# A perceiver block on one core: experts multiplied ahead of the next transposes, settling transposes pinned, and splits moved at both ends of the way up

## The chip, the core and the metric

The kernel runs on 1 core of one Trainium2 chip. The metric is the device time of one execution in microseconds (us), here the median of three runs. The engines are TensorE (PE, with its weight loads as PEld), VectorE (DVE), ScalarE (ACT), GpSimd (POOL) and SyncE (SP, which issues most DMAs).

## What is computed

One block in float32: a cross attention onto a masked context, a causal self attention with low-rank queries and keys, and a feed-forward part. 32 sequences of 64 tokens, 512 features.

```python
x = x + xattn(layernorm(x), ctx, mask)
x = x + attn(layernorm(x), ...)        # 16 heads; ends with out.reshape(..., 2048) @ wo.T + bo
h = layernorm(x)
y = square(relu(h @ up_w)) @ down_w    # 512 -> 2048 -> 512
y = y + (h @ expert_weight) * top2_sum(h @ gate_w)
x = x + layernorm(y) * ln_gamma + ln_beta
```

The matrix product of the attention's output with `wo` is called the way out, `h @ up_w` the way up and `... @ down_w` the way down. `expert_weight` and `gate_w` side by side are "the expert".

## The kernel before

**Tiling.** The 2048 tokens are 8 blocks of 256 (`NB`, `TB`). The three large products (way out, way up, way down) are made with seven products of submatrices in place of eight: sums of submatrices are formed on POOL, and each float32 operand is split into a high part (rounded to float32r, an ACT copy, L147) and a low part (the rest, a DVE subtraction, L149). A product of two split operands takes three matmuls: high x high, low x high, high x low. `split` does the pair of instructions and takes `pins`: an ACT and a DVE instruction behind which the two are issued. `after(ins)` orders the instructions of a block behind `ins` on its engine; it adds no semaphore. The order on each engine is otherwise a scheduler's, which follows the program's order by priority and issues ahead what it holds ready.

**The way out** runs over 64 units (`out_units`): a unit is one (block, k) and one call of `seven`, 21 matmuls of 128x256 (L723, L725, L726). k goes over the eight weight slots in the order of `ORDER`. `read_pair` reads a unit's operand with a DMA into one of the rooms of `ccp`, up to four units ahead; `left(u)` splits it into one of three `hl` rooms, two units ahead. `put_slot(k, "wo" | "up" | "down")` splits a weight into its slot (two ACT and two DVE instructions). At a block's last k its four PSUM banks are summed by `combine` (ACT L160, DVE L162 to L168), then `o_sum` and `o_norm` take the layer norm; POOL takes the root (L127), DVE writes `on` (L139).

**Transposes and experts.** `o_t(blk)` turns a normed block with eight transposes (L985) in two PSUM rooms of the pool `ps_t`, which has four rooms, and splits it into `oh` and `ol`; both have one room. It also copies it to `oT`, which ACT's queue stores to `xT_d` for the way up. `o_expert(blk)` multiplies `oh`, `ol` with the expert by `mm3` (L179 to L181): two halves of 128 tokens, each 12 matmuls of 264 columns and 12 of 256, 48 matmuls in four rooms of `ps_t`. DVE takes the two largest gate values (L1016) and adds them (L1018), ACT scales both parts into `mo` (L1021, L1022) and issues the store of `mo` to `mo_d` (L1023). `o_expert` is a generator: its first `yield` stands before the second half's scaling. Before, `o_t` for blocks 0 to 6 comes after the units in `TURN_AT`, `o_expert` after those in `MULT_AT`. Block 7's `o_t` and `o_expert` follow the loop.

**The rooms.** `o_act` (`ap`) holds `beb`, `mo`, `xt`, `o`, `p1`, `xn`, `oh`, `ol`, one room each, placed in the order of their first allocation. `mos` allocates `mo` ahead of the loop. When the way out ends, `pc.close()` frees the pool, and `f_act` (`fp`) is placed over it: three rooms for `uo`, the sums of the way up, and two for `p1`. A write to a new room waits until the tiles that lay there are done with.

**The way up** runs over 4 rounds (b, 512 tokens each) and in each over the 8 weights of `ORDER`: `up_seven` is 42 matmuls (L1156) into the four banks of one of two PSUM pools, then `combine`, ReLU and square on ACT (L1226, L1227), sums on POOL, stores to `h_d`. The first eight settling transposes are issued by `settle` (L713): transposes of 128 columns whose result is overwritten. `right(b, part)` splits the features of a round; round 0's four parts are split at the end of the way out and just behind it. The first weights of the way up are split inside the way out: `UP_PUT` names the units of block 7 after which `ORDER[0]` and `ORDER[1]` are split; `ORDER[2]` follows the last `o_t`; the others come in round 0, three weights ahead.

**The end of the way up and the way down.** In the last round the weights of the way down are split (`ORDER[n - 2]` for n = 2 to 6) and its first three operands by `left(0)`, `left(1)`, `left(2)` at n = 3, 5 and 6. The way down is again 64 units of 21 matmuls; `left(u + 3)` runs three units ahead. Four settling transposes stand after unit 4 and after unit 31 (`SETTLE_AT`), pinned behind the unit before (`ends`).

Of the kernel before, what the change touches and what calls it, by code (L numbers as in the profile page):

```python
# [9 lines left out]
FP = mybir.dt.float32  # L10
# [39 lines left out]

BARE_FIRST, BARE_LAST = ORDER[:5], ORDER[2:]

READ_AT, SLOT_AT = (1, 2, 4, 5), (3, 5, 7, 9, 11)
EXPERT_AT = (15, 16, 17, 18)
TURN_AT = (19, 22, 28, 34, 42, 50, 58)
MULT_AT = (21, 25, 31, 39, 47, 55, 63)

FEATURES_AT = (2, 4)
UP_READ, UP_PUT = (1, 2, 5, 6, 7), (3, 5)

BETA_AT = 60

# [24 lines left out]
def perceiver_block(ctx: ExitStack, tc: tile.TileContext, x, mem, mask, wq_a, bq_a, qnw, wq_b, bq_b,  # L87
# [53 lines left out]
    def after(ins):  # L141
        return tc.issue_after(ins.ins) if ins is not None else ExitStack()
# [32 lines left out]
    def mm3(ps, pairs):  # L175

        n = len(pairs)
        for j, (ah, al, bh, bl) in enumerate(pairs):
            nc.tensor.matmul(ps, ah, bh, start=(j == 0), stop=False)  # L179
            nc.tensor.matmul(ps, al, bh, start=False, stop=False)  # L180
            nc.tensor.matmul(ps, ah, bl, start=False, stop=(j == n - 1))  # L181


    with ExitStack() as mla:
# [409 lines left out]
        with ExitStack() as pb:  # L594
# [57 lines left out]
            def put_slot(k, what, pins=(None, None)):  # L652

                hl, c, _ = read_slots.pop((what, k))
                h, l = hl or room_of(k, what)
                for a in (slice(0, 4), slice(4, 7)):
                    split(h[:, a], l[:, a], c[:, a], pins=pins)
                wts[k] = (h, l)
# [342 lines left out]

    def o_expert(blk, xh, xl, _):

        mo = mos.pop(blk, None) or ap.tile([P, 2, D], FP, tag="mo", name=f"mo{blk}")
        for tt in range(2):
            i = 2 * blk + tt
            sl = slice(tt * P, (tt + 1) * P)
            pes = []
            for c in (slice(256, NE), slice(0, 256)):
                pe = ps_t.tile([P, D], FP, tag="T", name=f"cpe{i}_{c.start}")  # L1010
                mm3(pe[:, 0 : c.stop - c.start], [
                    (xh[:, k, sl], xl[:, k, sl], wes[0][:, k, c], wes[1][:, k, c]) for k in range(NKD)
                ])
                pes.append(pe)
            t8 = sp.tile([P, 8], FP, tag="t8", name=f"t8{i}")
            nc.vector.max(t8, pes[0][:, 256:264])  # L1016
            gs = sp.tile([P, 1], FP, tag="gs", name=f"gs{i}")
            nc.vector.tensor_tensor(gs, t8[:, 0:1], t8[:, 1:2], ALU.add)  # L1018
            if tt:
                yield  # L1020
            nc.scalar.mul(mo[:, tt, 256:512], pes[0][:, 0:256], gs)  # L1021
            nc.scalar.mul(mo[:, tt, 0:256], pes[1][:, 0:256], gs)  # L1022
        nc.scalar.dma_start(mo_d[blk], mo)  # L1023
        yield

    xr, xc, xw = {}, {}, []

    def read_x(b, kk, room=None, behind=None):

# [37 lines left out]
                    ins = nc.scalar.copy(t[:, to], src)  # L1067
        return ins

    mos = {0: ap.tile([P, 2, D], FP, tag="mo", name="mo0")}  # L1070
    put_slot(ORDER[2], "wo")
    xt, xns, xT, x2s, dones, read = {}, {}, {}, {}, {}, 5
    for u, (blk, k) in enumerate(out_units):
# [38 lines left out]
            put_slot(ORDER[UP_PUT.index(u % 8)], "up", pins=low)  # L1112
        if u in TURN_AT:
            i = TURN_AT.index(u)
            xT[i] = o_t(i, xns.pop(i))
            if i == 0:
                xns[1] = o_norm(1, *xns[1], low[1])
# [8 lines left out]
                xt[blk + 1] = o_load(blk + 1)  # L1126
        if u == BETA_AT:
            o_beta(NB - 2, low[1], nc.gpsimd)
        if u in MULT_AT:
            i = MULT_AT.index(u)  # L1130
            scaled = o_expert(i, *xT.pop(i))
            next(scaled)
            if i < NB - 2:
                next(scaled)
    xT = o_t(NB - 1, xns.pop(NB - 1), lambda: next(scaled))
    for part in range(3):
        right(0, part, (dones[NB - 1][0], xT[2][1]))
    put_slot(ORDER[2], "up", pins=xT[2])
    for _ in o_expert(NB - 1, *xT):
        pass  # L1140
    pc.close()


# [2 lines left out]
    with ExitStack() as pu:  # L1146
# [3 lines left out]
        def up_seven(ps, k, b, n, steps):  # L1150
            wh, wl = (t[:, 0:7].rearrange("p a (k f) -> p a k f", k=2) for t in wts[k])

            def product(s, parts, first=False, last=False):
                i, j = SEVEN[s]
                for m, (kk, w, low) in enumerate(parts):
                    nc.tensor.matmul(  # L1156
                        ps[s // 2][:, s % 2], w[:, i, kk], xr[b, 2 * kk + low][:, j],
                        start=(first and m == 0), stop=(last and m == len(parts) - 1),
                    )

            most = [(0, wh, 0), (0, wl, 0), (0, wh, 1), (1, wh, 0), (1, wl, 0)]
            rest = [(1, wh, 1)]
            one, two = (0, 2, 4, 6), (1, 3, 5)
            late = None
            if n == 0:
                with after(settle(8, ps, wh[:, 0, 0], ident2, None) if b == 0 else None):
                    for s in one:
                        product(s, most, first=True)
            if n == 7:
                for s in one:  # L1170
                    product(s, rest, first=True)
                for s in (0, 2, 4):
                    product(s, most, last=True)
                for s in two:
                    product(s, rest, first=True)
                if b + 1 < NB // 2:
                    late = right(b + 1, 3)
            for s in range(7):
                if n == 0 and s in one:
                    product(s, rest, last=True)  # L1180
                elif n < 7:
                    product(s, most + rest, True, True)
                elif s in two or s == 6:
                    product(s, most, last=True)
                if s in (1, 3, 5, 6):
                    with after(late if s == 3 else None):
                        next(steps)
# [8 lines left out]
                nc.sync.dma_start(h_d[b][:, k, 3:7], w)  # L1196

        stores = []
        right(0, 3)
        behind = read_slot(ORDER[5], "up", behind=reads[-1])  # L1200
        for b in range(NB // 2):
            if b == NB // 2 - 1:
# [2 lines left out]
            for n, k in enumerate(ORDER):  # L1205
# [28 lines left out]
                    summed = sums(at, LEFT)  # L1234
                if b == 0 and n < 5:
                    put_slot(ORDER[n + 3], "up", pins=pins)
                if b == NB // 2 - 1 and 1 < n < 7:
                    put_slot(ORDER[n - 2], "down", pins=pins)
                if b == NB // 2 - 1 and n == 2:
                    for u in range(2):  # L1240
# [2 lines left out]
                    left(0, pins=(done[0], done[-1]))  # L1243
                if b == NB // 2 - 1 and n == 5:
                    left(1, pins=(done[0], done[-1]))
                if b == NB // 2 - 1 and n == 6:
                    left(2, pins=(done[0], done[-1]))
                if b == NB // 2 - 1 and n == 7:
                    read_pair(5, from_h)
                if stores and (b, n) != (NB // 2 - 1, 7):  # L1250
# [8 lines left out]
    with ExitStack() as pd:  # L1259
# [82 lines left out]
        for u, (blk, k) in enumerate(out_units):  # L1342
            if k == ORDER[0]:
                pss[blk] = banks(ps_f[DOWN.index(blk) % 2], f"dp{blk}")
            while read <= min(max(u + READ_AHEAD, 2 * u + 1), u + READ_FAR, last_unit):
                read_pair(read, from_h, room_for(read))
                read += 1
            for v in [v for v in bares if v <= u + SUM_AHEAD]:
                c = bares.pop(v)
                with after(pows[-1]):  # L1350
                    sums([c[:, 6]] + [c[:, d] for d in range(7)], LEFT)
# [14 lines left out]
                store_h(*stores.pop(0))  # L1366
            if u == 6:
                nc.sync.dma_start(gab, gamma.partition_broadcast(P))
            if u in (4, 6, 8):
                put_slot(ORDER[3 + u // 2], "down")  # L1370
            if u in (2, 4):
                read_slot(ORDER[5 + u // 2], "down")
            outs = [d for d in outs if step(d, low)]
# [52 lines left out]
```

## Time and profile before

| | us |
|---|---|
| median of 3 runs | 1103.37 |
| lowest and highest run | 1101.33, 1103.40 |
| the profiled execution's own time | 1098.9 |
| its span, first to last instruction | 1096.7 |
| attention and folding, 0 to about 551 | 551 |
| way out, about 551 to 773.1 | 222 |
| way up, 773.1 to 931.2 | 158 |
| way down and the end, 931.2 to 1096.7 | 165 |

In the stretch 553 to 773 PE is busy 212.9 of 220 us, from 773 to 931.2 157.6 of 158.2, and from there to the end 155.5 of 165.5, of which the last ten are the output's tail on DVE and ACT. The granted clock is 1.00 in all three.

Rows of a list of groups, a list of waits or an order of time read: start (us), duration, engine, line, operation, out<-in by the program's names, partitions x elements, count, and in brackets the idle time of that engine before it with what ended it. A row of a stretch reads: from:to, its length, the busy time of PE with the number of instructions that touch the stretch, then the granted clock, the DMA engines' share and GB/s. Matmul ends are modelled and matmuls overlap, so their starts are what tells a pace.

### The profile page before, as it was taken

What the parts mean: (1) busy time and instruction counts of PE and PEld (TensorE: products, weight loads), DVE (VectorE), ACT (ScalarE), POOL (GpSimd) and SP (SyncE); (2) the same over time, 40 slices, a digit from 0 to 9 for tenths busy, and PEclk for the clock granted to TensorE, in tenths of its full rate; (3) what the DMA queues carried; (4) which work ended last, traced back from release to release, by engine and by line L of the source; (5) the groups of instructions that cost most, each with busy time, mean ns of one, the idle gap of its engine ahead of it and who ended that gap; (6) DMA issues with size and microseconds to landing.
All of it is one profiled execution on the core that took longest, in us unless ns stands there. A gap on an engine that the chain in (4) does not pass through costs nothing.

```text
span 1096.7 us, 26072 instructions
## 1 busy us (share of the span) xinstructions
PE 1066.9 (97%) x10201; PEld 983.6 (90%) x10201; DVE 769.0 (70%) x1369; ACT 546.1 (50%) x1051; POOL 508.1 (46%) x691
## 2 busy tenths in 40 slices
PE   8999999999999999999998999999999999999996
PEld 6667777679999999999988999999999999999996
DVE  5666666657666666656787866667785658898786
ACT  4444444533433444434475544445676567755553
POOL 2333333326788778874570000003238970065671
PEclk9999999999999999999999999999999999999999
DMA  8867666343776778655487776779646689998672
GB/s 259 263 216 231 206 212 203 124 161 121 260 234 245 260 247 294 249 207 195 160 324 276 263 241 213 231 235 359 218 156 202 221 247 366 310 309 257 206 232 79
DMA packets 195386, 254.67 MB, mean 232 GB/s; under 512 B 18544, under 2 KB 140032, under 8 KB 195264
## 3 DMA queue, kind: packets, MB, share of 16 engines
q1 hardware_dynamic: 190704, 240.92, 67.0%
q10 hardware_dynamic: 3456, 8.39, 2.2%
q0 software_dynamic: 1104, 3.70, 0.9%
q8 instruction: 80, 1.31, 0.5%
q14 instruction: 42, 0.34, 0.1%
HBM read 146.67 MB, written 106.30 MB: 231 GB/s over the span
## 4 chain that ended last, share of the span: by engine, by line
PE 59%; DMA 10%; POOL 9%; DVE 8%; issue 7%; ACT 5%; SPq 1%; DVEq 0%; POOLq 0%; ACTq 0%
PE up L1156 9%; PE pss L773 5%; PE psq L179 4%; PE psq L180 4%; PE psq L181 4%; PE op L725 3%; PE op L726 3%; PE op L723 3%; PE psv L817 3%; DMA hd<-uo 2%; PE pse L179 2%; PE pse L181 2%; PE pse L180 2%; DMA x1d<-xt 2%; DMA vd<-vw 2%
## 5 line engine op out<-in xcount | busy, mean ns | idle before, releaser
L755 DVE SCALAR_TENSOR_TENSOR qe<-pse,bqp,cq 64x256 f32<-64x256 f32 x256 | 123.7, 483 | 76.5 <-PE pse L181 70.7
L1156 PE MATMUL up<-xr,wh_up 128*128 128x256 f32 x896 | 157.6, 280 | 0.6 <-DVE uo L168 0.6
L1156 PEld LDWEIGHTS up<-xr,wh_up 128*128 128x128 f32 x896 | 137.5, 189 | 1.0 <-issue 0.7
L725 PE MATMUL op<-wh_wo,hl 128*128 128x256 f32 x448 | 124.4, 279 | 3.7 <-DVE hl L149 3.7
L723 PE MATMUL op<-wh_wo,hl 128*128 128x256 f32 x448 | 124.0, 280 | 0.6 <-ACT hl L147 0.6
L725 PE MATMUL dp<-wh_down,hl 128*128 128x256 f32 x448 | 124.5, 278 | 0.0
L723 PE MATMUL dp<-wh_down,hl 128*128 128x256 f32 x448 | 124.4, 278 | 0.0
L726 PE MATMUL dp<-wl_down,hl 128*128 128x256 f32 x448 | 124.3, 277 | 0.0
L149 DVE TENSOR_TENSOR hl<-c,hl 128x896 fp32r<-128x896 f32 x84 | 94.3, 1126 | 42.3 <-ACT hl L147 42.0
L1156 PE MATMUL up<-xr,wl_up 128*128 128x256 f32 x448 | 123.7, 280 | 0.0
L726 PE MATMUL op<-wl_wo,hl 128*128 128x256 f32 x448 | 123.5, 277 | 0.0
L147 ACT CAST hl<-c 128x896 fp32r<-128x896 f32 x84 | 79.0, 942 | 77.7 <-PE op L726 38.0
L179 PE MATMUL psq<-qa_hi,qh 128*128 128x256 f32 x384 | 112.5, 293 | 0.0
L180 PE MATMUL psq<-qa_hi,ql 128*128 128x256 f32 x384 | 106.4, 277 | 0.0
L181 PE MATMUL psq<-qa_lo,qh 128*128 128x256 f32 x384 | 106.2, 276 | 0.0
L725 PEld LDWEIGHTS op<-wh_wo,hl 128*128 128x128 f32 x448 | 84.3, 188 | 4.8 <-DVE hl L149 4.7
L723 PEld LDWEIGHTS op<-wh_wo,hl 128*128 128x128 f32 x448 | 83.6, 188 | 1.5 <-ACT hl L147 0.8
L723 PEld LDWEIGHTS dp<-wh_down,hl 128*128 128x128 f32 x448 | 84.6, 189 | 0.0
L725 PEld LDWEIGHTS dp<-wh_down,hl 128*128 128x128 f32 x448 | 84.1, 188 | 0.4 <-DVE hl L149 0.4
L1156 PEld LDWEIGHTS up<-xr,wl_up 128*128 128x128 f32 x448 | 84.2, 188 | 0.0
L726 PEld LDWEIGHTS op<-wl_wo,hl 128*128 128x128 f32 x448 | 84.1, 188 | 0.0
L726 PEld LDWEIGHTS dp<-wl_down,hl 128*128 128x128 f32 x448 | 84.1, 188 | 0.0
(233 smaller groups left out, 3146.6 us busy)
## 6 DMA issues: line engine op xcount, KB each, us to landing
c<-vd SPq DMA_DIRECT2D x58, 448.0 KB, 4.2
cx<-in_ctx SPq DMA_DIRECT2D x32, 512.0 KB, 4.6
vd<-vw SPq DMA_DIRECT2D x29, 512.0 KB, 3.6
hd<-uo SPq DMA_DIRECT2D x107, 128.0 KB, 3.3
hd<-uw SPq DMA_DIRECT2D x21, 512.0 KB, 3.3
dcw<-hd SPq DMA_DIRECT2D x18, 448.0 KB, 5.6
vd<-v SPq DMA_DIRECT2D x30, 256.0 KB, 3.5
wd_wo<-pw_wo SPq DMA_DIRECT2D x8, 896.0 KB, 4.9
```

The costliest lines, as they stand in the source:

```text
L147: copy = nc.scalar.copy(hi, src)
L149: return copy, engine.tensor_tensor(lo, src, hi.bitcast(FP), ALU.subtract)
L179: nc.tensor.matmul(ps, ah, bh, start=(j == 0), stop=False)
L180: nc.tensor.matmul(ps, al, bh, start=False, stop=False)
L181: nc.tensor.matmul(ps, ah, bl, start=False, stop=(j == n - 1))
L723: first = nc.tensor.matmul(ps[s // 2][:, s % 2], h[:, a], wh[:, b], start=(k == 0 and s % 2 == 0), stop=False)
L725: nc.tensor.matmul(ps[s // 2][:, s % 2], l[:, a], wh[:, b], start=False, stop=False)
L726: ins = nc.tensor.matmul(ps[s // 2][:, s % 2], h[:, a], wl[:, b], start=False, stop=last)
L755: rope = nc.vector.scalar_tensor_tensor(qe[64 * a : 64 * a + 64, :], pe[r, :], bqp[r, p : p + 1], cq[r, a, :], ALU.add, ALU.mult,)
L773: nc.tensor.matmul(ps[64 * j : 64 * j + 64, pj, b, :], qs[2 * pj + j][a][:, sl], kT[:, a, kt], start=(a == 0), stop=(a == 1),)
L817: nc.tensor.matmul(o, kv[a, i, :], t[a, bp, :], start=True, stop=True)
L1156: nc.tensor.matmul(ps[s // 2][:, s % 2], w[:, i, kk], xr[b, 2 * kk + low][:, j], start=(first and m == 0), stop=(last and m == len(parts) ...
```

## The change

- `mos` goes: `mo` is allocated when the first `o_expert` runs.
- `MULT_AT` goes: `o_expert(i - 1)` runs whole directly ahead of `o_t(i)` for i = 1 to 6; block 6's stays after the last unit, its last scaling still between block 7's transposes and their copies.
- `ORDER[1]` of the way up is no longer split after the sixth unit of block 7 but behind the first three `right` parts: its ACT half pinned to the last `left`'s ACT copy, its DVE half to the last `o_t`'s low part. `ORDER[2]` moves from there to behind the fourth part, `right(0, 3)`.
- The way up's settling transposes become four, issued behind the last matmul of the last expert (`made[-1]`, kept as `ends`; `mm3` returns its last matmul).
- In the last round of the way up `ORDER[4]`'s split and `left(2)` go; `left(2)` is issued at unit 0 of the way down ahead of the others, `ORDER[4]` after unit 1.

```diff
-UP_READ, UP_PUT = (1, 2, 5, 6, 7), (3, 5)
+UP_READ, UP_PUT = (1, 2, 5, 6, 7), (3,)
-MULT_AT = (21, 25, 31, 39, 47, 55, 63)
...
-            nc.tensor.matmul(ps, ah, bl, start=False, stop=(j == n - 1))
+            ins = nc.tensor.matmul(ps, ah, bl, start=False, stop=(j == n - 1))
+        return ins
...
-        mo = mos.pop(blk, None) or ap.tile([P, 2, D], FP, tag="mo", name=f"mo{blk}")
+        mo = ap.tile([P, 2, D], FP, tag="mo", name=f"mo{blk}")
...
-                mm3(pe[:, 0 : c.stop - c.start], [
+                made.append(mm3(pe[:, 0 : c.stop - c.start], [
...
-    mos = {0: ap.tile([P, 2, D], FP, tag="mo", name="mo0")}
...
         if u in TURN_AT:
             i = TURN_AT.index(u)
+            if i:
+                for _ in o_expert(i - 1, *xT.pop(i - 1)):
+                    pass
             xT[i] = o_t(i, xns.pop(i))
...
-        if u in MULT_AT:
-            i = MULT_AT.index(u)
-            scaled = o_expert(i, *xT.pop(i))
+        if u == last_unit:
+            scaled = o_expert(NB - 2, *xT.pop(NB - 2))
             next(scaled)
-            if i < NB - 2:
-                next(scaled)
     xT = o_t(NB - 1, xns.pop(NB - 1), lambda: next(scaled))
     for part in range(3):
         right(0, part, (dones[NB - 1][0], xT[2][1]))
-    put_slot(ORDER[2], "up", pins=xT[2])
+    put_slot(ORDER[1], "up", pins=(low[0], xT[2][1]))
     for _ in o_expert(NB - 1, *xT):
         pass
+    ends = made[-1]
...
-                with after(settle(8, ps, wh[:, 0, 0], ident2, None) if b == 0 else None):
+                with after(settle(4, ps, wh[:, 0, 0], ident2, ends) if b == 0 else None):
...
-        right(0, 3)
+        put_slot(ORDER[2], "up", pins=(xT[2][0], right(0, 3)))
...
-                if b == NB // 2 - 1 and 1 < n < 7:
+                if b == NB // 2 - 1 and 1 < n < 6:
                     put_slot(ORDER[n - 2], "down", pins=pins)
...
-                if b == NB // 2 - 1 and n == 6:
-                    left(2, pins=(done[0], done[-1]))
...
+            if u == 0:
+                left(2)
...
-            if u in (4, 6, 8):
-                put_slot(ORDER[3 + u // 2], "down")
+            if u in (1, 4, 6, 8):
+                put_slot(ORDER[max(4, 3 + u // 2)], "down")
```

`settle`, which the change calls with another count and pin, is unchanged:

```python
def settle(n, ps, sta, one, behind):
    for i in range(n):
        with after(behind):
            behind = nc.tensor.transpose(ps[3][:, 1, 0:P], sta.bitcast(FP), one)
    return behind
```

More of the change, by code (lines that the diff above doesn't have):

```diff
@@ L1010, in o_expert @@
                 pe = ps_t.tile([P, D], FP, tag="T", name=f"cpe{i}_{c.start}")
-                mm3(pe[:, 0 : c.stop - c.start], [
+                made.append(mm3(pe[:, 0 : c.stop - c.start], [
                     (xh[:, k, sl], xl[:, k, sl], wes[0][:, k, c], wes[1][:, k, c]) for k in range(NKD)
-                ])
+                ]))
                 pes.append(pe)
@@ L1024, in o_expert @@
         yield
-    xr, xc, xw = {}, {}, []
+    xr, xc, xw, made = {}, {}, [], []
     def read_x(b, kk, room=None, behind=None):
```

## The prediction

> **What bounds the kernel now.** I read the page first, then TensorE's busy time in equal stretches, then the order of time on each engine round the edited places.
>
> ```profile
> span 1096.7 us, 26072 instructions
> PE 1066.9 (97%) x10201; PEld 983.6 (90%) x10201; DVE 769.0 (70%) x1369; ACT 546.1 (50%) x1051; POOL 508.1 (46%) x691
> ```
>
> TensorE (PE) sets the time. So an edit is worth only the PE waits that it ends, the matmuls it adds, or a change of the pace at which matmuls follow each other. That pace isn't constant. The next view counts the up matmuls (128x256) in four stretches of 33 us, with the granted clock at 1.00 in all:
>
> ```profile
> 774.00:807.00 33.00, 33.00 (x283) 1.00 0.46 147
> 811.00:844.00 33.00, 33.00 (x294) 1.00 0.61 203
> 850.00:883.00 33.00, 33.00 (x283) 1.00 0.63 206
> 896.00:929.00 33.00, 33.00 (x282) 1.00 1.07 355
> ```
>
> One matmul lasts 0.28 us and the edges count too, so a stretch is 33.28 us: 33.28/283 = 117.6 ns from start to start, against 33.28/294 = 113.2 ns. There are two paces, 4.4 ns apart. The order of time shows where they turn: 117.6 ns from 773.1 to the PE wait at 808, 113.2 to three short waits at 846.8 to 847.5, then 117.6 through the rest of the way up and five units of the way down, to 943.5. There four settling transposes stand, and behind them 532 matmuls take 60.28 us, 113.3 ns each. A wait can leave either pace behind it; the transposes of the way out and of the way down were each followed by the quick one.
>
> **The start of the way up.** The kernel issues eight settling transposes there, and they aren't where they would help:
>
> ```profile
> 764.82 1.08 PE L985 MATMUL ops<-ident,on 128*128 128x128 f32 x8 [1.02 <-DVE on L139]
> 765.75 0.49 PE L713 MATMUL up<-ident,wh_up 128*128 128x128 f32 x3
> 766.66 0.51 PE L179 MATMUL cpe<-we_hi,oh 128*128 128x264 f32 x2 [0.43 <-ACT oh L147]
> 767.01 0.60 PE L713 MATMUL up<-ident,wh_up 128*128 128x128 f32 x4
> 773.04 0.27 PE L713 MATMUL up<-ident,wh_up 128*128 128x128 f32 x1
> 773.07 0.36 PE L1156 MATMUL up<-xr,wh_up 128*128 128x256 f32 x1
> ```
>
> Seven ran inside or ahead of the last expert, in time that PE was waiting anyway; one stands before the first up matmul. The change issues four, behind the expert's last matmul. The four at 943.53 cost 0.36 us to the next matmul's start (943.89) and the row after it starts 0.20 instead of 0.12 us later, so about 0.11 each: three more on the path, **+0.3** (bounds 0 and +0.45). If they leave the quick pace, the 297 matmuls up to 808 gain 4.4 ns each, **-1.3** (bounds 0, if one more disturbance follows, and -1.3).
>
> The Trainium skill speaks against this part: "TensorE: Matmul & The Clock Gate", section "Back-to-back issue gap", gives a warm isolated gap of N/2.4 + 2.5 ns, 109 ns for 256 columns, as a single value. By that rule no transpose could change the pace, and this part would only cost its 0.3. The trace has 113.2 and 117.6 at a granted clock of 1.00, so the rows decide.
>
> **The room of the first sums.** `mo` is allocated second in `o_act` before, so the first `uo` of the way up lies over it. The change allocates `mo` last there. In the trace:
>
> ```profile
> 774.17 0.33 ACTq L1023 DMA_DIRECT2D mod<-mo  x1
> 780.10 0.69 DVE L162 TENSOR_TENSOR uo<-up,up 128x512 f32<-128x512 f32 x1 [4.67 <-ACT up L160]
> 808.87 0.48 PE L1156 MATMUL up<-xr,wh_up 128*128 128x256 f32 x2 [0.57 <-DVE uo L168]
> ```
>
> The store of the last `mo` takes 5.8 us to land, so 779.97. DVE then starts its first sum of the way up at 780.10, though PE had ended that sum's banks at about 777.3 (34 matmuls after 773.07, 0.118 each, and the last one's end). The page names ACT's copy, which came late by chance; the wait is for the store. Behind it DVE runs a cycle of 4.73 us per weight (its splits at 785.37, 790.10, 794.83, 799.56, 804.29), PE one of 42 x 117.6 = 4.94, or 4.75 at the quick pace. DVE is therefore never more than level, and the late start is still there at 808.02, where PE waits 0.85 - 0.11 = 0.74 us. Starting about 3 us sooner, while PE gains 1.3 on it, DVE has 1.7 in hand against the 0.74. **-0.7** (bounds 0 and -0.74). What is late next are ORDER[1]'s and ORDER[2]'s low halves, both moved behind the last transposes. On DVE a low half is 1.2 + 0.95 us; they fit in the 4.67 us of idle that stood there, and ORDER[1]'s ends about when the way up begins, 4.75 us before its second weight needs it.
>
> **The end of the way out.** ORDER[1]'s low half runs on DVE at 755.37 (2.63 us, two instructions), and the last block's first sum follows at 757.92. PE had ended the banks for it at about 757.0. Sum, norm and POOL's root hang on it, and the last transposes waited 1.02 us for `on`. With the split pinned behind the transposes the chain starts 0.9 sooner: **-0.9** (bounds 0 and -1.0, the whole wait).
>
> **Experts ahead of the transposes.** All 8 x 48 expert matmuls and 8 x 8 transposes stay; only their order against the units changes. Two waits go:
>
> ```profile
> 617.44 0.51 PE L179 MATMUL cpe<-we_hi,oh 128*128 128x264 f32 x2 [0.47 <-ACT oh L147]
> 755.50 0.39 PE L725 MATMUL op<-wh_wo,hl 128*128 128x256 f32 x1 [0.63 <-DVE hl L149]
> ```
>
> At 616.70 expert 0 waited for its own split (0.74 to the next start against 0.12): it now stands behind the rest of that unit, **-0.6**. At 754.60 a pair landed late (its read issued at 746.48 took 6.82 us). That read waited for a room that the split of unit 61 frees, and that split for unit 58's matmuls. Before, an expert of 5.76 us stood in front of units 56 to 58; now it stands behind them, so the read goes out about 5.8 us sooner against the same need: 0.90 - 0.11, **-0.8** (bounds +0.9, if a run of eight units without a pause meets a late pair elsewhere, and -0.8). The moved stores of `mo` stay on ACT's queue, ahead of the casts that follow the transposes; these casts have eight units of cover.
>
> **The end of the way up.** ORDER[4]'s split (DVE 2.1, ACT 1.8) and left(2) (1.08 and 0.94) leave the last block and come as first work of the way down (the pair for left(2) is still read at the old place, into its own room, and only holds it longer). In the stretch 931.2 to 943.4 DVE is busy 11.5 and ACT 11.7 of 12.2 us, so this is no free place: left(2) is due two units (4.8 us) in, and my queue of DVE ends it 0.5 us before; ORDER[4] is due 9.5 us in, and ends about 0.4 before. At the slow pace **0**; at the quick pace PE arrives 1.5 us sooner and could wait 1 to 1.5 us in all.
>
> **What the waits leave behind.** The second round (b = 1) ends with short waits: these six matmuls take 1.23 us, where five paces of 0.113 and one end of 0.28 are 0.85, so 0.38 is waiting.
>
> ```profile
> 846.59 1.23 PE L1156 MATMUL up<-xr,wh_up 128*128 128x256 f32 x6
> 943.53 0.60 PE L713 MATMUL dp<-ident,wh_down 128*128 128x128 f32 x4
> ```
>
> They come from POOL and ACT work of that round, which keeps its place relative to PE; I expect them again, and behind them either pace. The 815 matmuls from there to 943.5 are slow now: quick would give -3.6, less up to 1.5 of new waits. Half of 2.1 gives **-1.0** (bounds +1.5, if the second round's 327 turn slow, and -3.6). The 250 slow matmuls of the way down from 1035 are a throw of the same kind, 1.1 either way; I take 0.
>
> **Sum.** +0.3 - 1.3 - 0.7 - 0.9 - 0.6 - 0.8 - 1.0 = -5.0 us against this execution, 1098.9 us with 2.2 outside the span. It lies 4.5 under the median of 1103.37 (1101.33 to 1103.4). 4.5 us is 1000 matmuls at the other pace, so other executions probably drew worse; I take the difference off the median: **1098.4**.
>
> **Rivals.** (1) *The quick pace holds from 773 to the way down*: nothing disturbs PE at 847. The throw then gives -3.6 in place of -1.0: 1095.8. For it: behind transposes the pace stayed for up to 567 matmuls; against: the waits at 847 are no part of the change. (2) *DVE and ACT take the gain of the way up back*: they run 4.73 us per weight against 4.75, so PE only arrives to wait. Then only -0.9 - 0.6 - 0.8 + 0.3 remain: 1101.4, no change that can be told. Against it: DVE idles 4.67 us at the start. (3) *Slower: the transposes wait for rooms*. `ps_t` has four rooms, an expert fills all four, and transposes now follow at once. They wait if the second scaling of the expert's first half ends later than its own 48 matmuls, 5.76 us. For expert 5 it ended at 736.34, 5.07 us after 731.27; for expert 0 at 624.34, 6.90 after 617.44. It decides against the change from 4.0/6 = 0.67 us late at each of six turns; at expert 0's 1.14 it costs 6.8, net 1103.37 - 5.0 + 6.8 = 1105.2. Against it: five of six new places have no block's end beside them, which is what delayed DVE in both rows. (4) *It doesn't do what it says*: the order within PE is set by a scheduler, which had already moved the eight settling transposes; but the four now have an edge to hold them. I count it within (2).
>
> **How the numbers follow.** Forecast 0.54, (1) 0.17, (2) 0.16, (3) 0.13. A difference under 0.2%, 2.2 us, can't be told from none here. Faster is the forecast and (1), 0.71, less a little for the forecast's own upper end: 0.69. Same takes (2) and that: 0.17; slower 0.14. The forecast's own range is 1095.5 to 1101.3; for 8 in 10 it goes down to 1094.3 (all terms at their best ends and a kind throw in the way down) and up to 1103.5 (the terms halved and the second round slow).
>
> **What would show it.** Four settling transposes directly ahead of the first up matmul, and 294 matmuls in the first 33 us of the way up; DVE's first `uo` sum about 4 us after the first up matmul instead of 7; no wait near its 297th matmul; the last transposes within 0.3 us of the expert; no waits of expert 0 on `oh` or of the last unit on a pair. I'm wrong if transposes show waits on `mo` scalings, if the pace behind the four is 117.6, or if new waits stand in the first five units of the way down.

## The result and the profile after

The changed kernel takes **1109.91 us** (median of 4 runs, 1108.5 to 1110.55) against 1102.58 for the kernel before (median of 4, 1101.33 to 1103.4). The ratio is **1.0072, 95% interval 1.0044 to 1.0099**: slower by 0.7%. The forecast was 1098.4 with a range up to 1103.5, so both its sign and its range were wrong. The profiled execution took 1109.55 us against 1098.9.

The first two lines of the page of the changed kernel, the span and the busy times:

```profile
span 1107.3 us, 26052 instructions
...
PE 1072.2 (97%) x10197; PEld 987.5 (89%) x10197; DVE 766.8 (69%) x1369; ACT 545.3 (49%) x1051; POOL 498.5 (45%) x691
```

No work was added: DVE and ACT are busy 2.2 and 0.8 us less than before. The 10.6 us of span are time in which TensorE stood still or ran slower. By stage, from first matmul to first matmul: the way out from the first transposes took 159.5 instead of 158.4 us, the way up 165.7 instead of 158.1, the rest 168.3 instead of 165.5; what lies ahead of the first transposes took 0.75 less. So 7.6 us of the loss are in the way up and 2.8 behind it. (The granted clock of the kernel before in its last stretch is 0.98, not 1.00: 1.00 up to 1086.5 and 0.74 in the output's tail.) TensorE's busy time in stretches of the changed kernel (from:to, length, busy time and instructions, granted clock, DMA share, GB/s; the busy times of the other engines stand between):

```profile
774.00:807.00 33.00, 32.99 (x291) 32.82 (x290) 26.29 (x44) 22.75 (x41) 5.77 (x8) 1.00 0.46 147
811.00:844.00 33.00, 30.09 (x256) 29.92 (x255) 21.81 (x39) 19.34 (x37) 27.46 (x34) 1.00 0.60 197
850.00:883.00 33.00, 33.00 (x282) 33.00 (x282) 20.52 (x37) 17.79 (x34) 26.83 (x35) 1.00 0.65 214
896.00:929.00 33.00, 29.81 (x241) 29.64 (x240) 18.68 (x33) 19.76 (x36) 10.17 (x14) 0.95 0.95 304
912.00:916.00 4.00, 3.71 (x19) 3.74 (x19) 3.68 (x9) 2.72 (x5) 2.26 (x4) 0.58 0.64 192
```

The first stretch has 291 matmuls where it had 283: the quick pace followed the settling transposes. The second and the fourth have some 27 and 42 fewer than a slow stretch, so there are holes in them, and behind the second hole the granted clock is 0.58 for 4 us (behind the first it stayed at 1.00). Rows of TensorE's order of time show all that was foreseen and the two holes that weren't:

```profile
764.79 1.09 PE L986 MATMUL ops<-ident,on 128*128 128x128 f32 x8 [0.30 <-DVE on L139]
766.63 0.51 PE L179 MATMUL cpe<-we_hi,oh 128*128 128x264 f32 x2 [0.75 <-ACT oh L147]
...
773.00 0.60 PE L714 MATMUL up<-ident,wh_up 128*128 128x128 f32 x4
773.36 0.37 PE L1157 MATMUL up<-xr,wh_up 128*128 128x256 f32 x1
...
814.88 0.35 PE L1157 MATMUL up<-xr,wh_up 128*128 128x256 f32 x1 [2.91 <-DVE uo L162]
...
912.29 0.36 PE L1157 MATMUL up<-xr,wh_up 128*128 128x256 f32 x1 [3.19 <-DVE up L163]
```

From start to start the two waits cost 3.19 - 0.11 = 3.1 us and 3.47 - 0.11 = 3.4. The 16 matmuls behind the second took 0.21 us each, 1.6 more. All waits in the way up grew from 0.74 to 6.85 us; with the 1.6 that is 7.7, against 7.6 measured. The pace has no part in it: 328 up matmuls are quick where 331 were.

**The wait at 811.7.** The second round's first weight needs the banks of the first round's seventh weight, so DVE must have begun that weight's sums. DVE's order of time in the changed kernel:

```profile
804.48 0.42 DVE L168 TENSOR_TENSOR uo<-uo,up 128x256 f32<-128x256 f32 x1
806.17 2.10 DVE L149 TENSOR_TENSOR wl_up<-wl_up,wh_up 128x1024 fp32r<-128x1024 f32 x2 [1.27 <-ACT wh_up L147]
...
811.41 1.06 DVE L1066 TENSOR_TENSOR xr<-xp,xr 128x768 fp32r<-128x768 f32 x1 [1.13 <-PE up L1157]
812.39 1.74 DVE L1066 TENSOR_TENSOR xr<-xc,xr 128x1024 fp32r<-128x1024 f32 x1
814.06 1.27 DVE L162 TENSOR_TENSOR uo<-up,up 128x512 f32<-128x512 f32 x2
```

and in the kernel before:

```profile
808.63 0.69 DVE L162 TENSOR_TENSOR uo<-up,up 128x512 f32<-128x512 f32 x1
...
811.39 1.13 DVE L1065 TENSOR_TENSOR xr<-xp,xr 128x768 fp32r<-128x768 f32 x1 [0.35 <-PE up L1156]
812.44 1.75 DVE L1065 TENSOR_TENSOR xr<-xc,xr 128x1024 fp32r<-128x1024 f32 x1
814.12 0.68 DVE L162 TENSOR_TENSOR uo<-up,up 128x512 f32<-128x512 f32 x1
```

The split of the second round's fourth part (L1065, now L1066) runs at the same time in both, because it waits for TensorE to leave the part's room. Before, the seventh weight's sums came ahead of it, at 808.63; now they come behind it, at 814.06 (x2: the seventh's and the eighth's). TensorE waits for the first of them. DVE idled 1.27 and 1.13 us meanwhile, so it wasn't full: its instructions stand in another order. ScalarE's order moved with it: its two copies for these sums (L160) start at 812.23, behind its half of the fourth part. Read from the traces, the first round's order on DVE, one symbol for each group (S n: the five sums of a weight, from S0 for the first to S7 for the eighth; s: only the first four; S n': the fifth; W: a weight's split; R: a part of the next round's features):

```
before  S0 s1 W S1' s2 W S2' s3 W S3' s4 W S4' s5 W R S5' S6 R(fourth) S7
after   S0 S1 W W S2 S3 W W S4+S5 W R R(fourth) S6+S7
```

**The wait at 908.8.** ScalarE's order of time in the changed kernel, and then in the kernel before:

```profile
898.14 0.35 ACT L160 COPY up<-up 128x256 f32<-128x256 f32 x1
907.63 0.94 ACT L147 CAST hl<-hl 128x896 fp32r<-128x896 f32 x1 [9.14 <-DMA hl<-hd]
...
910.56 0.62 ACT L160 COPY up<-up 128x256 f32<-128x256 f32 x2
```

```profile
911.85 0.35 ACT L160 COPY up<-up 128x256 f32<-128x256 f32 x1
912.11 0.94 ACT L147 CAST hl<-hl 128x896 fp32r<-128x896 f32 x1
912.99 0.37 ACT L160 COPY up<-up 128x256 f32<-128x256 f32 x1
```

DVE's order of time in the changed kernel:

```profile
908.60 1.09 DVE L149 TENSOR_TENSOR hl<-hl 128x896 fp32r<-128x896 f32 x1 [7.62 <-ACT hl L147]
911.00 0.69 DVE L162 TENSOR_TENSOR uo<-up,up 128x512 f32<-128x512 f32 x1 [1.31 <-POOL uw L155]
```

The cast at 907.63 waits for the last of three reads from `h_d`, issued at 899.56 and landed at 907.60. It is `left(2)`. It was written as first work of the way down, without pins, and its read had always been issued here. In the kernel before, with pins, its cast ran at 928.50: the move that was to make it later made it 21 us earlier. ACT and DVE now take its split ahead of the second weight's sums of the last round and stand 9.14 and 7.62 us for its data. ScalarE's squares of the first weight, for which POOL waits, and its two copies at 910.56, which the sums need, come behind the cast. TensorE needs the banks of the second weight again for the fourth, at 908.8.

### The profile page after: what moved, and what is told of

Its sections match the earlier page's. It is cut to its first block, busy times and chain, and to the rows that moved or that the text cites. A ratio compares the mean times of both kernels' runs of the same rounds, so it can differ in the third digit from the quotient of the medians.

```text
span 1107.3 us, 26052 instructions
## 1 busy us (share of the span) xinstructions
PE 1072.2 (97%) x10197; PEld 987.5 (89%) x10197; DVE 766.8 (69%) x1369; ACT 545.3 (49%) x1051; POOL 498.5 (45%) x691
## 3 DMA queue, kind: packets, MB, share of 16 engines
q8 instruction: 80, 1.31, 0.5%
```

## The experiments

Every ratio is against the kernel before in the same batch, with its 95% interval. The way up is from its first matmul to the way down's first in the one profiled execution.

| kernel | median us | ratio | way up, us |
|---|---|---|---|
| before | 1102.58 | 1 | 158.1 |
| changed | 1109.91 | 1.0072 [1.0044, 1.0099] | 165.7 |
| e1_split_behind_expert | 1105.05 | 1.0022 [1.0003, 1.0041] | 163.0 |
| e2_pair_pinned | 1107.18 | 1.0048 [1.0030, 1.0066] | 162.5 |
| e3_both | 1102.37 | 0.9993 [0.9978, 1.0007] | 156.2 |
| e4_before_split_moved | 1108.42 | 1.0056 [1.0038, 1.0075] | 163.7 |
| h1_end_alone | 1107.96 | 1.0036 [1.0022, 1.0049] | 162.7 |
| f3_rooms_settle_alone | 1100.59 | 0.9986 [0.9970, 1.0002] | 156.8 |
| f4_experts_alone | 1104.65 | 1.0010 [0.9990, 1.0030] | 158.9 |
| f1_end_as_before | 1098.95 | 0.9969 [0.9953, 0.9985] | 157.6 |
| f2_end_pinned | 1099.46 | 0.9974 [0.9962, 0.9986] | 156.0 |
| g1_p1_first | 1100.22 | 0.9978 [0.9963, 0.9992] | 156.0 |
| g2_settle_each_round | 1103.65 | 1.0008 [0.9990, 1.0026] | 155.9 |
| g3_experts_as_before | 1101.16 | 0.9987 [0.9970, 1.0005] | 156.3 |

**Undoing the order.** In e1_split_behind_expert one line changes place:

```diff
-    put_slot(ORDER[1], "up", pins=(low[0], xT[2][1]))
     for _ in o_expert(NB - 1, *xT):
         pass
+    put_slot(ORDER[1], "up", pins=(low[0], xT[2][1]))
```

> The changed kernel with one line moved: the split of the second up weight is written behind the last expert instead of ahead of it, with the same two pins. No work is added or removed. In VectorE's program the first round of the way up goes back from pairs (sum, sum, split, split) to one split inside each weight's sums. Theory (order): the 3.19 us wait of TensorE at 811.7 came from the paired order, so it goes; the 3.47 us wait at 908.8 stays. 3.1 off the changed kernel's 1109.9: 1106.8, and down to 1103.3 if the 796 matmuls behind the wait then keep the quick pace (4.4 ns each). Rival (DVE is simply full): the first sum still starts late behind the store of oT, and at the quick pace TensorE outruns the splits in either order; the wait at 811 stays at 2.5 us or more and the time within 1 us of 1109.9.

In e2_pair_pinned `left(2)` gets pins, and in e3_both both edits are made:

```diff
-                left(2)
+                left(2, pins=(done[0], done[-1]))
```

> The changed kernel with pins on left(2) alone: its two halves may not start before the sums of the last weight of the way up. Theory (order): the split was taken by ScalarE and VectorE ahead of the sums of weight 1 of the last round, where its read from HBM (issued 899.56, landed 907.60) held both engines; pinned, the wait of 3.47 at 908.8 and the stretch at clock 0.58 behind it go: 3.4 + 1.5 = 4.9 off 1109.9, 1105.0; the wait at 811.7 stays. Rival (the end of the way up is too full): the split then comes due at the first units of the way down and the same 3 us are waited there; time within 1.5 us of 1109.9.

> Both edits of the two other kernels of this batch at once. Theory (order): both 3 us waits go; 1109.9 - 3.1 - 4.9 = 1101.9, and down to 1098.4 if the quick pace then holds from 773 to 908. Rival (full engines): 1107 or more, with waits near 811 or at the first units of the way down.

DVE's order of time in e1_split_behind_expert has the seventh weight's sums (808.49) ahead of the fourth part again, and TensorE has no wait there; its wait near 908 stays:

```profile
808.49 0.68 DVE L162 TENSOR_TENSOR uo<-up,up 128x512 f32<-128x512 f32 x1
...
811.30 1.06 DVE L1066 TENSOR_TENSOR xr<-xp,xr 128x768 fp32r<-128x768 f32 x1 [0.42 <-PE up L1157]
```

```profile
910.98 0.48 PE L1157 MATMUL up<-xr,wh_up 128*128 128x256 f32 x1 [3.44 <-DVE up L163]
```

In e2_pair_pinned it is the other way round: no wait over 0.2 us between 819 and 938, and the first one unchanged (TensorE's order of time):

```profile
818.79 0.36 PE L1157 MATMUL up<-xr,wh_up 128*128 128x256 f32 x1 [2.91 <-DVE uo L162]
```

e1's median lies within the 1103.3 to 1106.8 that the theory of the order gave it; e2's is 2.2 above its 1105.0. The pace isn't the reason, for e2's way up has as many slow matmuls as the changed kernel's, 991. But behind e2's wait the granted clock fell, where behind the changed kernel's wait of the same 3.19 us it had not, and 17 matmuls took about 0.21 us, 1.6 us more in this execution:

```profile
818.79:822.79 4.00, 4.00 (x22) 4.00 (x23) 3.63 (x9) 2.26 (x5) 0.51 (x1) 0.60 0.80 266
```

For these two waits the rivals (full engines) are out: the same instructions in another order have no wait. e3_both, at 1102.37, has neither wait and some 1330 up matmuls at 113.4 ns, but a third wait shows where its rival had looked for one, at the beginning of the way down. TensorE's row, then DVE's:

```profile
933.80 0.36 PE L724 MATMUL dp<-wh_down,hl 128*128 128x256 f32 x1 [2.87 <-DVE up L163]
```

```profile
931.50 0.68 DVE L162 TENSOR_TENSOR uo<-up,up 128x512 f32<-128x512 f32 x1
932.10 1.22 DVE L149 TENSOR_TENSOR wl_down<-wl_down,wh_down 128x1024 fp32r<-128x1024 f32 x1
933.24 0.41 DVE L163 TENSOR_TENSOR up<-uo,up 128x256 f32<-128x256 f32 x1
```

The way down's first banks come free with the sum at 933.24, and a `wl_down` split stands in the middle of the sums: with `ORDER[4]` written behind the way up, unpinned, DVE's last splits were ordered anew too. That split is 1.0 of the 3.0 us; the sums themselves began only at 931.50, behind another weight's split, when TensorE's last up matmul had started at 930.65.

**Each part alone.** e4_before_split_moved is the kernel before with only `ORDER[1]`'s split moved:

```diff
-UP_READ, UP_PUT = (1, 2, 5, 6, 7), (3, 5)
+UP_READ, UP_PUT = (1, 2, 5, 6, 7), (3,)
...
+    put_slot(ORDER[1], "up", pins=(low[0], xT[2][1]))
     put_slot(ORDER[2], "up", pins=xT[2])
```

> The kernel before with one part of the change alone: the second up weight's split moved behind the last transposes (from unit 61), same pins as in the change; eight unpinned settling transposes, experts and rooms as before. Theory (order): this part alone puts the first round's sums and splits into pairs, and a wait of about 3 us appears at the start of the second round; the last transposes' wait on DVE shrinks by about 0.7: 1102.6 + 3.1 - 0.7 = 1105.0. Rival (the pairs are harmless, the wait came from the freed rooms or from the quick pace): no wait over 1 us near 811, 1101.9.

```profile
817.86 0.36 PE L1157 MATMUL up<-xr,wh_up 128*128 128x256 f32 x1 [3.28 <-DVE uo L162]
```

```profile
814.40 1.05 DVE L1065 TENSOR_TENSOR xr<-xp,xr 128x768 fp32r<-128x768 f32 x1 [1.14 <-ACT xr L1067]
815.38 1.74 DVE L1065 TENSOR_TENSOR xr<-xc,xr 128x1024 fp32r<-128x1024 f32 x1
817.04 1.27 DVE L162 TENSOR_TENSOR uo<-up,up 128x512 f32<-128x512 f32 x2
```

TensorE's wait and the order of DVE's three rows are those of the changed kernel, from this one moved split, without freed rooms and without pinned transposes. (The fourth part waited last for ScalarE's half of it here, which had stood behind squares, and not for TensorE.) It is slower than expected (1108.42 against 1105.0): in its profiled execution two more waits of 0.6 us (at 793 and 803), one of 1.2 us (at 774.8, for a part of the features) and one of 0.5 (at 919) stand in its way up, and behind the wait at 814.3 the granted clock is 0.65 over 4 us, 1.6 us more.

h1_end_alone is the kernel before with only its end changed:

```diff
-                if b == NB // 2 - 1 and 1 < n < 7:
+                if b == NB // 2 - 1 and 1 < n < 6:
                     put_slot(ORDER[n - 2], "down", pins=pins)
...
-                if b == NB // 2 - 1 and n == 6:
-                    left(2, pins=(done[0], done[-1]))
...
+            if u == 0:
+                left(2)
...
-            if u in (4, 6, 8):
-                put_slot(ORDER[3 + u // 2], "down")
+            if u in (1, 4, 6, 8):
+                put_slot(ORDER[max(4, 3 + u // 2)], "down")
```

> The kernel before with one part of the change alone, the lighter end of the way up: left(2) and the fifth down weight's split moved to the way down, both without pins as in the change. Theory (order): left(2)'s split is taken ahead of the sums of weight 1 of the last round and waits there for its read: a wait of TensorE of about 3.4 us at its third weight, near 906, with a stretch at a lower clock behind it (1.5); and the fifth weight's split between the last two sums adds 0.4 to 2.9 at the way down's start: 1102.6 + 3.4 + 1.5 + 0.4 = 1107.9, up to 1110. Rival (as the change means it, and as the prediction counted it, nothing): 1102.6 within 1.5, no wait over 1 us between 900 and 935.

TensorE's wait and ACT's cast:

```profile
912.26 0.55 PE L1156 MATMUL up<-xr,wh_up 128*128 128x256 f32 x1 [2.68 <-DVE up L163]
```

```profile
907.60 0.94 ACT L147 CAST hl<-hl 128x896 fp32r<-128x896 f32 x1 [8.64 <-DMA hl<-hd]
```

So this part alone makes the second hole, and costs 0.36%. A wait that costs 1.4 us at the way down's beginning (937.5) is e3_both's place again.

f3_rooms_settle_alone (no `mos`, four settling transposes behind the last expert) and f4_experts_alone (`o_expert(i - 1)` ahead of `o_t(i)`) are the two parts that leave DVE's order in the way up as it was:

> The kernel before with two parts of the change alone: no second room of mo, and four settling transposes pinned behind the last expert in place of eight unpinned ones. VectorE's program is that of before. Theory (as in the prediction): four transposes directly ahead of the first up matmul, quick pace behind them, DVE's first sum of the way up earlier than 7 us after the first up matmul, no wait near the 297th: -2.0 + 0.3, 1101. Rival: the first sum now waits for the store of oT (as in the changed kernel, 5.3 us after the first up matmul), the wait near the 297th comes back in the quick pace and ends it: 1102.6.

> The kernel before with one part of the change alone: each expert multiplied directly ahead of the next transposes. Theory (as in the prediction): expert 0's wait on oh (0.6) and the late pair at 754.6 (0.8) go: 1101.2. Rival 1: the scheduler splits each expert round three units in the trace of the changed kernel (its first 11 to 16 matmuls, then 63 of the units, then the rest), so its first waits and the transposes' waits on the mo scalings (0.4 us each) take the gain back: 1102 to 1103. Rival 2 (the pace): the units that follow the transposes directly were quick before and turn slow where expert matmuls follow them, 82 matmuls x 4.4 ns a turn, four turns: +1.4, 1103 to 1104.

f3 reached its 1101, though its interval just includes no change; its first sum came 4.5 us after the first up matmul, there was no wait near the 297th, and the quick pace ran from about 784 to 852. f4 gained nothing: expert 0's wait and the late pair are gone, but 660 of the way out's matmuls were quick where 854 had been (194 x 4.4 ns = 0.9 us). In the trace the first matmuls of an expert come ahead of three units (or five) and the rest behind them, and from the third expert on those units run slow. That is its second rival in kind and about two thirds of its size.

The four parts add up (`ORDER[2]`'s move, the fifth, wasn't run alone): -0.14 + 0.56 + 0.10 + 0.36 = +0.88%, each known to 0.13 to 0.20, against +0.72% (0.44 to 0.99) for all together.

**A version without the two orders.** f1_end_as_before is the changed kernel with e1's moved line and the old end of the way up; f2_end_pinned is e3_both with `ORDER[4]` pinned as well:

```diff
-                put_slot(ORDER[max(4, 3 + u // 2)], "down")
+                put_slot(ORDER[max(4, 3 + u // 2)], "down", (pins if u == 1 else (None, None)))
```

> The changed kernel with the second up weight's split written behind the last expert, and with the end of the way up as in the kernel before (left(2) and the fifth down weight's split back in the last round). Rooms, settling transposes, experts and the third weight's split stay changed. Theory (order): neither of the two 3 us waits, and none of the 2.87 us that e3_both showed at 930.65, where the fifth weight's split stood between the two last sums of the way up in VectorE's program; the quick pace (113.4 ns) can hold from 778 to 930 as in e3_both. e3_both less 2.9 and less the 17 matmuls at 0.21 us behind that wait (1.7): 1097.8, up to 1100 if TensorE, 5 us ahead at the quick pace, meets VectorE full at the end. Rival (the end is full whatever the order, which is why the change lightened it): a wait of 2 us or more at the way down's start again, 1102.

> e3_both with the fifth down weight's split pinned too, behind the last sums of the way up, as left(2) is. Theory (order): with both pins the end of the way up is really lighter on VectorE; the 2.87 us wait at its end goes, and what was pinned comes due at units 2 and 4 of the way down: waits there of up to 0.5 us each. 1097.8, up to 1099. Rival (the work only moves): left(2) and the split are late at units 2 and 4 by 1 us or more each, and the time is e3_both's, 1102.

Both beat both kernels: **f1 at 0.9969 (0.9953 to 0.9985), f2 at 0.9974 (0.9962 to 0.9986)**. DVE's order in f1 has the seventh weight's sums (806.12) ahead of the fourth part (808.94):

```profile
806.12 0.68 DVE L162 TENSOR_TENSOR uo<-up,up 128x512 f32<-128x512 f32 x1
...
808.94 1.06 DVE L1066 TENSOR_TENSOR xr<-xp,xr 128x768 fp32r<-128x768 f32 x1 [0.42 <-PE up L1157]
...
811.60 0.68 DVE L162 TENSOR_TENSOR uo<-up,up 128x512 f32<-128x512 f32 x1
```

f1 lies inside what the theory gave it, f2 0.5 us above. f2 kept an idle time of 1.31 us at the way down's start and one of 0.64 at 957, so its lighter end is worth nothing above f1's: there its rival was half right, the work mostly moved.

g3_experts_as_before is f1 with the experts at their old places:

> f1_end_as_before with the experts back at their old places, three to eight units behind the transposes. Theory (the experts' move costs in the pace what it gains in waits): the runs of 164 quick matmuls between experts come back (840 quick ones in the way out against 609: 1.0 us), and so do expert 0's wait on oh (0.4 to 0.8) and the late pair near 755 (0.8 to 2.5): time within 1 us of 1098.95. Rival 1 (the prediction's step: the move is worth 1.4): 1100.3. Rival 2 (the move is a loss): 1097 or less.

Its 1101.16 can't be told from f1's; the quick matmuls (831 in the way out) came back and so did waits of 1.4 us on expert 0 and 1.5 on the late pair. Whether the move helps stays open within 2 us.

**The pace.** g1_p1_first swaps two allocations of f1, and g2_settle_each_round adds transposes to g1:

```diff
-                o = fp.tile([P, 5, TB], FP, tag="o", name=f"uo{b}_{k}")
                 p1 = fp.tile([P, TB], FP, tag="p1", bufs=2, name=f"up1_{b}_{k}")
+                o = fp.tile([P, 5, TB], FP, tag="o", name=f"uo{b}_{k}")
```

```diff
-                with after(settle(4, ps, wh[:, 0, 0], ident2, ends) if b == 0 else None):
+                with after(settle(4, ps, wh[:, 0, 0], ident2, ends if b == 0 else None)):
```

> f1_end_as_before with the two allocations at the head of each up weight's sums swapped: p1 before uo, so p1 lies over the room of beta instead of that of oT, whose store held ScalarE's first copy until 5.47 us after the first up matmul. Theory (rooms): the first sum starts within 4.4 us of the first up matmul, and the wait near the 297th matmul (0.33 at 805.75 in f1_end_as_before, after which the pace was 117.8 for 1156 matmuls) goes; the quick pace from the settling transposes then has no wait to end it before the second round: 0.5 to 3 us off f1_end_as_before's 1098.95: 1096 to 1098.5. Rival (DVE's cycle of 4.73 us per weight sets it whatever the start): the wait comes anyway, and the time is 1098.95 within 1.

> g1_p1_first with four settling transposes ahead of every round of the way up instead of the first alone: 12 more transposes of about 0.11 us, 1.3 us on the path. Theory (transposes set the quick pace, waits end it): each round starts at 113.4 ns per matmul; of 1344 up matmuls at least 1200 are quick against 294 in f1_end_as_before, 4 us against 1.3: net 2 to 3 us below it where it was slow, 1096. Rival (the pace is a property of the whole execution or of what DVE and ACT do at the time, and transposes only coincide with it): slow stretches stand behind the transposes of rounds 2 to 4, and the time is 1.3 above g1_p1_first.

Stretches within the rounds of the way up, first of g1 (rounds 2 and 3), then of g2 (rounds 2, 3 and 4):

```profile
811.00:844.00 33.00, 33.00 (x294) 33.00 (x293) 19.08 (x34) 20.42 (x38) 28.88 (x37) 1.00 0.62 203
850.00:883.00 33.00, 33.00 (x283) 33.00 (x282) 18.36 (x34) 19.10 (x35) 29.72 (x38) 1.00 0.62 204
```

```profile
820.00:853.00 33.00, 33.00 (x294) 33.00 (x293) 19.00 (x37) 20.56 (x37) 26.07 (x35) 1.00 0.67 223
860.00:893.00 33.00, 33.00 (x283) 33.00 (x282) 18.92 (x36) 19.04 (x35) 28.07 (x37) 1.00 0.71 225
900.00:933.00 33.00, 33.00 (x294) 33.00 (x293) 23.54 (x40) 23.69 (x43) 8.36 (x12) 1.00 1.05 344
```

Both missed what the theory gave them (1096 to 1098.5, and 1096). In g1 the way up has no wait over 0.2 us, but three matmuls at 845.5 to 846.2 follow each other at 0.25, 0.24 and 0.23 us, and behind these short waits the pace turns from 113.4 to 117.8 ns. Three such short waits stand at this place, the first matmuls of the second round's last weight, in eight of the ten kernels that come there at the quick pace: behind them it is 117.8 in before, h1, f3, f4, g1 and g3, and 113.4 still in e3 and f2. (e4 and g2 have no wait there and no turn.) In g2 four transposes stand directly ahead of the third round (855.90) and the pace behind them is 117.8. So transposes and short waits often come with a change of pace, but neither settles it. The twelve transposes bought nothing: the way up took 155.9 us against 156.0. What sets the pace is open.

g2's median is 3.4 us above g1's all the same. Its twelve transposes are TensorE's, yet the order on ScalarE and DVE changed where the way down begins. ScalarE takes the cast of another down weight, for whose data it stands 2.46 us, ahead of the casts of the next operands; in g1 it comes behind them. DVE's split of the operand that TensorE needs (943.61) comes late. Rows of ScalarE's, DVE's and TensorE's order of time in g2:

```profile
936.23 1.05 ACT L147 CAST wh_down<-wl_down 128x1024 fp32r<-128x1024 f32 x1 [2.46 <-DMA wl_down<-wd_down]
...
940.34 2.10 DVE L149 TENSOR_TENSOR wl_down<-wl_down,wh_down 128x1024 fp32r<-128x1024 f32 x2 [1.17 <-ACT wh_down L147]
...
943.61 1.09 DVE L149 TENSOR_TENSOR hl<-c,hl 128x896 fp32r<-128x896 f32 x1
...
944.75 0.58 PE L726 MATMUL dp<-wh_down,hl 128*128 128x256 f32 x1 [2.25 <-DVE hl L149]
```

With the slower clock behind it this wait costs some 4 us in the profiled execution, the slowest of g2's twelve.

## Why the prediction was wrong, point by point

- **The room of the first sums**: the step that failed. It put the cost of `ORDER[1]`'s moved split at nothing because the low halves of `ORDER[1]` and `ORDER[2]` "fit in the 4.67 us of idle that stood there". That counted the moved instructions and took the order of all others as given. The move made the scheduler pair the first round's sums and splits, and the seventh weight's sums fell behind a split that waits for TensorE itself: 3.1 us in the changed kernel, +0.56% alone (e4), gone when the line is moved behind the last expert (e1). The rest of this step held in part: the wait at 808 (0.74) went, though f1 has one of 0.5 us there again. The first sum came 5.0 us after the first up matmul, not 4, for `p1` now lies over `oT`, whose store held ACT's copy until 777.9; that cost nothing that g1 could show.
- **The end of the way up**, put at 0 because both splits "come as first work of the way down", failed in the same way: the unpinned `left(2)` came some 30 us ahead of the way down and 21 us earlier than in the kernel before, ahead of its own data, 3.4 + 1.6 us (h1: +0.36% alone).
- **Rival (4)**, that the scheduler's order isn't the written one, was counted inside "no change" at most. It was the case, with another sign. Rival (3) named the slower side, but with transposes that wait for `ps_t`: in the changed kernel that happened once, 0.39 us at 624.44. (Its 4.0/6 leaves out the term of -1.0; with the whole 5.0 it is 0.83 us at each turn.)
- **The start of the way up**: right. Four transposes at 773.00, quick pace behind, 0.36 us to the first up matmul. The quick pace followed in all ten kernels with the four pinned transposes, and in one (h1) of the four with the eight unpinned ones; but four transposes didn't bring it in g2's third round.
- **The end of the way out**, -0.9: about -0.2. The wait on `on` fell from 1.02 to 0.30, but the last expert's first matmuls then waited 0.75 for `oh` and 0.22 for `ol` where it had been 0.43, ACT's cast being behind the scaling of `mo`.
- **Experts ahead of the transposes**, -1.4: the waits went as foreseen (expert 0, 754.6), one of 0.39 took their place, and the pace of the units in between took back 1.0 (636 quick matmuls in the way out against 854). The term lacked the pace, which the same text had priced elsewhere.
- **What the waits leave behind**, -1.0: wrong in this execution. The three short waits at 847 on which the term hung did not come: from the new wait at 811.7 on the way up was slow already, for 990 matmuls. The way down had 675 quick ones against 973 (+1.3) and 1.7 us of waits. That either pace can follow those waits, as the term had it, the eight kernels above show.

With the two orders undone, f1 came to 1098.95, near the forecast's 1098.4. In part that is luck: the experts' term gained nothing that could be told (f4), the last term was a throw, and f1 keeps the old end of the way up. The terms are not confirmed one by one; f3 and f4, the two parts that leave the order alone, come to -0.04% together, known to about 0.26, against f1's -0.31%. What the runs show is that the loss came from the order of other work, which the sum left out.

## What to carry to other kernels

Where a scheduler orders the engines, an edit is not priced by the instructions that it moves: one moved split re-ordered the sums and splits of a whole round, and it took no added work to lose 3 us. Even transposes added on TensorE (g2) came with another order on DVE and ACT. Before pricing, set the order of each engine before and after the edit side by side, and look for a wait that now stands ahead of work TensorE needs. An instruction that depends on a transfer and has no pin can be taken long ahead of where it is written; a move meant to make something later must pin it there.

## What was not expected of the hardware

- **The clock after a short wait.** Behind TensorE waits of 2.5 to 3.7 us (start to start: g2 2.53, h1 2.96, e3 3.15, e2 3.19, changed at 908.8 3.47, e4 3.56, e1 3.73) the granted clock was 0.57 to 0.65 over the next 4 us, and matmuls took 0.21 us; behind waits of 1.6 (f2, f4) it stayed at 1.00, and behind the changed kernel's 3.19 at 811.7 too. The Trainium skill, "TensorE: Matmul & The Clock Gate", in its Part 1 on the HAM clock gate, has the clock halved after an idle window of about 3.4 us and full again after as long a busy one, the window running freely. The length of the slow stretch agrees: half clock for about 3.4 of 4 us gives the 0.57. That 2.5 us of waiting can be enough, and 3.19 once was not, the runs show beside it. So a 3 us wait can cost some 1.6 us more than itself.
- **Two paces at full clock.** In the profiles of all fourteen kernels matmuls of 256 columns follow each other at 113.4 or 117.8 ns for hundreds in a row; some 1330 of the way up ran quick in e3_both, and some 1150 in a row slow in f1, from 806 into the way down. All of the way up and the way down at the one pace or the other makes 2688 x 4.4 ns = 11.8 us. Executions of one kernel in the experiments spread by 3 to 10 us (f1: 1094.93 to 1104.08). How much of that is the pace no run shows; in f1 and g2 the slower executions also have the lower mean clock (f1: 0.998 in the fastest of twelve, 0.993 in the slowest).
